# Causal attentions: queries and keys projected without padding, and spread to padded rows by a round trip through DRAM

## The chip, the cores and the metric

The kernel runs on one core of a Trainium2 chip. The metric is the device time of one execution in microseconds (us). TensorE (PE) multiplies matrices, VectorE (DVE), ScalarE (ACT) and GpSimd (POOL) do the rest of the arithmetic, and SyncE (SP) issues DMAs. Each engine runs its own instruction stream in order; semaphores order them among each other.

## The reference

The kernel computes a decoder of two layers on 16 sequences of 512 positions, with model width D = 256 and 16 heads of 16 numbers each. Every sub-layer adds its result to `x` and normalises. Layer 0: a causal self-attention with a learned position term, a cross attention to 64 context rows, and a mixture of ten experts. Layer 1: a causal self-attention with low-rank projections, a cross attention with one head, and a feed-forward part. The two causal attentions, cut to what matters:

```python
# layer 0
q, k, v = jnp.split(x @ Wqkv.T, 3, axis=-1)              # 16 heads of 16
logits = jnp.einsum('bhqd,bhkd->bhqk', q, k) * scale
logits = logits + _fourier_bias(alpha, beta, t)[None]    # sum_r alpha cos(w_r (i-j)) + beta sin(w_r (i-j))
attn = softmax(where(causal, logits, -inf)); out = (attn @ v) @ Wout.T
# layer 1
q = x @ wq_lat @ wq_heads;  k = x @ wk_lat @ wk_heads    # 256 -> 64 -> 256
att = softmax(where(causal, q k^T * SCALE, -inf));  y = (att @ v) @ w_proj + b_proj
```

The position term of layer 0 depends on i - j through cosines and sines, so it is an inner product of 16 position features of the query with 16 mixed features of the key.

## The kernel before

Everything is kept in float32 apart from masks and a split of the row maxima. The weights are loaded once; then 16 sequences pass through four stages each: `a0` (causal attention of layer 0), `d0` (first cross attention and experts), `a1` (causal attention of layer 1) and `d1` (second cross attention and feed-forward).

**Order of the work.** The code first records operations with `op(engine, cost, emit, reads, writes, wait)` (line 288): an engine, an estimated cost, and the buffers (`Slot`) they touch. `run_plan` (line 346) then lists them: at each step it takes the operation that can start earliest by its own clock, and among those that could start within 0.02 us on one engine the one with the lowest rank (line 395). The rank is the stage's place plus the fraction of its PE cost that is done, with 0.5 taken off for what touches an attention's buffers (line 325). The places (line 402) put `a1` of one sequence beside `d0` of the next, and `d1` beside `a0` of the one after, so that the dense stages fill PE while an attention waits. The plan's order is written into each engine's stream: `pe`, `dve`, `act` and `pool` are `Pinned` (line 344), which keeps the program's order on that engine. DMAs on `nc.sync` are not pinned before the change: `x`, `ctx` and `mi` are loaded by `inputs` (line 1366), and the result stored at line 1398.

**Heads and padding.** Attention scores are matmuls that contract over 32 rows of the array, one head to a strip of 32 partitions, four heads (a group) to a tile of 128 partitions. A head has 16 numbers, so 16 of 32 rows are its own; in layer 0 the other 16 hold the position features (`qfeat` for the query, a product with `kmat` for the key), in layer 1 row 16 carries the row maximum in the query and -1 in the key (`onerow`), and the rest is zero.

`queries_keys(g)` makes the two padded tiles `q` and `k` [128, 512] of group g. In `attention0` (line 825) the weight `wqk0` holds zero columns for the padding: two matmuls (two chunks of the 256 contraction rows) for the query, DVE scales it and adds `qfeat` (line 833); two matmuls and a third with `kmat` and `qfeat` (line 841) for the key, ACT copies it out. In `attention1` (line 869) one matmul each from the 64 latent rows, on the two halves of the array, with ACT scaling the query and adding the -1 row to the key. A matmul of 512 float32 columns stands in the trace as two records.

`causal_attention` (line 557) works a group in two passes: units of maxima (q against k, masked, reduced by DVE into `m`), then units of exponentials (k against q, `exp` on ACT, the triangle cut on POOL), and their products with the values. It calls `queries_keys(g)` two units of maxima ahead of the group's first (line 750); the tiles come from pools of three buffers (line 264). Its own large buffers come from `a4` with two buffers, so that one attention starts when the former is nearly done.

## Time and profile before

| | us |
|---|---|
| median of 3 runs | 4504.14 (4497.92 to 4506.57) |
| profiled execution | 4507.05 |
| its span, first to last instruction | 4505.3 |
| PE busy | 4260.3 (95%) |
| DVE busy | 2641.7 (59%) |
| ACT busy | 1571.0 (35%) |
| POOL busy | 1205.5 (27%) |
| mean granted PE clock | 0.988 of full speed |

Busy time of PE is the union of its matmuls' spans; the spans overlap in the pipeline, so what one matmul takes from the next is read from start to start. A group of instructions is named out<-in by the program's tiles: `pq` and `pk` are the PSUM tiles of the projections, `pa` the scores, `po` the products with the values, `pt` transposes, `pg`, `pu` and `pe` the experts. All recorded operations stand under line 340, the helper that pins them, so the tile names tell them apart. DMA rows give the issuing queue, how many there were, KB each, and the median time from issue to landing.

One sequence takes about 272 us in the middle of the run: its attention1 starts at 876.7, 1148.5 and 1421.9 us for three sequences in a row.

### The profile page before, as it was taken

The page shows a single profiled execution, that of the slowest core. Times are in us where ns is not written, and L with a number is a line of the kernel's source. Part 1 is how long each engine was busy: PE and PEld are TensorE (multiplying, and loading weights), DVE is VectorE, ACT ScalarE, POOL GpSimd, SP SyncE. Part 2 cuts the span into 40 slices and gives each one's busy share as a digit, 9 for nine tenths or more (in the row PEclk, how much of TensorE's full clock was granted, in tenths as well). Part 3 has the DMA queues.
Part 4 walks back from the last instruction along what each step waited for, and adds up shares of the span by engine and source line. Part 5 has one row for each costly group of instructions (what it writes and reads, how often), then busy time and mean ns, then how long its engine had stood idle before and what let it go on. Part 6 is the DMA issues. An engine that isn't in the chain of part 4 may idle for free.

```text
span 4505.3 us, 65388 instructions
## 1 busy us (share of the span) xinstructions
PE 4260.3 (95%) x26816; PEld 2372.9 (53%) x26816; DVE 2641.7 (59%) x5317; ACT 1571.0 (35%) x2273; POOL 1205.5 (27%) x2221
## 2 busy tenths in 40 slices
PE   4999999999999999999999999999999999999897
PEld 2455555555555555555555555555555555555544
DVE  2456566565666556665565665656665565655554
ACT  1323242434314243242433414343242432424333
POOL 0313231323313133131322313233131332313322
PEclk8999999999999999999999999999999999999998
DMA  4000000000000000000000000000000000000000
GB/s 129 2 1 1 2 10 2 10 1 2 10 2 10 1 2 10 2 10 1 11 1 2 10 2 10 1 2 10 2 10 1 6 6 1 10 1 6 1 1 10
DMA packets 41355, 35.05 MB, mean 8 GB/s; under 512 B 11424, under 2 KB 39904, under 8 KB 41056
## 3 DMA queue, kind: packets, MB, share of 16 engines
q1 hardware_dynamic: 30736, 23.70, 1.7%
q10 hardware_dynamic: 10320, 7.17, 0.5%
q8 instruction: 211, 3.46, 0.3%
q14 instruction: 88, 0.72, 0.1%
HBM read 22.47 MB, written 8.39 MB: 7 GB/s over the span
## 4 chain that ended last, share of the span: by engine, by line
PE 84%; ACT 6%; DVE 5%; POOL 2%; issue 1%; DMA 1%; SPq 0%; ACTq 0%; POOLq 0%; DVEq 0%
PE pa L340 22%; PE pf L340 8%; PE pq L340 7%; PE pg L340 7%; PE pe L340 6%; PE pu L340 6%; PE po L340 6%; PE pp L340 5%; PE pk L340 4%; ACT e L340 4%; PE pt L340 4%; PE ps L340 3%; PE pv L340 3%; DVE m L340 2%; PE pl L340 1%
## 5 line engine op out<-in xcount | busy, mean ns | idle before, releaser
L340 DVE TENSOR_REDUCE m<-pa 128x2 f32<-128x1024 f32 (+3 forms) x1024 | 805.6, 818 | 425.7 <-PE pa L340 423.5
L340 ACT ACTIVATE e<-pa 128x1024 f32<-128x1024 f32 (+1 forms) x768 | 662.6, 884 | 685.9 <-PE pa L340 647.7
L340 PE MATMUL pa<-q,k 32*128 32x512 f32 (+3 forms) x4096 | 665.5, 472 | 23.0 <-ACT e L340 19.7
L340 POOL TENSOR_SCALAR_AFFINE_SELECT e<-e 128x256 f32<-128x256 f32 x1024 | 437.9, 441 | 918.1 <-ACT e L340 906.8
L340 PE MATMUL pa<-k,q 32*128 32x512 f32 (+3 forms) x4096 | 616.6, 471 | 51.3 <-DVE m L340 40.2
L340 PEld LDWEIGHTS pa<-k,q 32*128 32x128 f32 x4096 | 271.4, 185 | 345.3 <-issue 155.0
L340 PEld LDWEIGHTS pa<-q,k 32*128 32x128 f32 x4096 | 297.2, 186 | 170.5 <-ACT e L340 67.3
L340 PE MATMUL po<-e,vp 128*32 128x512 f32 (+3 forms) x4096 | 360.5, 447 | 18.0 <-POOL e L340 15.9
L340 ACT ACTIVATE h<-pg 128x512 f32<-128x512 f32 x160 | 95.5, 597 | 708.2 <-PE pg L340 708.2
L340 POOL TENSOR_TENSOR rs<-rs,minus_half 128x2 f32<-128x2 f32 x192 | 133.4, 716 | 708.3 <-DVE rs L340 707.6
L340 PE MATMUL pe<-w,h 128*128 128x256 f32 x1280 | 307.6, 381 | 0.8 <-DVE h L340 0.8
L340 PE MATMUL pg<-xT,w 128*128 128x512 f32 x640 | 303.9, 597 | 0.0
L340 PE MATMUL pu<-xT,w 128*128 128x512 f32 x640 | 301.8, 594 | 0.0
L340 PEld LDWEIGHTS pe<-w,h 128*128 128x128 f32 x1280 | 240.6, 190 | 97.2 <-issue 59.0
L340 PE MATMUL pf<-xT,L_ffn_W 128*128 128x512 f32 x512 | 248.3, 610 | 0.2 <-ACT xT L340 0.2
L340 POOL CAST parts<-m 128x16 bf16<-128x16 f32 x192 | 55.2, 288 | 711.4 <-DVE m L340 703.2
L340 DVE SCALAR_TENSOR_TENSOR x<-pe,r_pick,x 128x256 f32<-128x256 f32 x512 | 215.5, 477 | 42.8 <-PE pe L340 42.8
L340 PE MATMUL pf<-ff,act 128*128 128x256 f32 x1024 | 235.7, 384 | 3.9 <-ACT act L340 3.9
L340 DVE SCALAR_TENSOR_TENSOR h<-h,pg 128x512 f32<-128x512 f32 x160 | 110.0, 687 | 197.9 <-ACT h L340 197.9
L340 PEld LDWEIGHTS <-ident 128*128 128x128 bf16 x1536 | 92.5, 97 | 245.3 <-issue 217.3
L340 PE MATMUL pa<-cmask,ident 128*128 128x128 bf16 (+1 forms) x1536 | 220.1, 242 | 0.0
L340 PEld LDWEIGHTS pf<-ff,act 128*128 128x128 f32 x1024 | 193.2, 192 | 37.4 <-ACT act L340 6.2
(180 smaller groups left out, 6359.9 us busy)
## 6 DMA issues: line engine op xcount, KB each, us to landing
x<-in_x SPq DMA_DIRECT2D x16, 512.0 KB, 3.9
out_x<-x SPq DMA_DIRECT2D x16, 512.0 KB, 2.9
wqk<-in_wqk ACTq DMA_DIRECT2D x1, 1024.0 KB, 6.0
w<-in_L_ffn_routed_w SPq DMA_DIRECT2D x8, 128.0 KB, 3.8
w<-in_L_ffn_routed_w ACTq DMA_DIRECT2D x8, 128.0 KB, 4.0
w<-in_L_ffn_routed_w ACTq DMA_DIRECT2D x1, 1024.0 KB, 9.6
L_ffn_W<-in_L_ffn_W SPq DMA_DIRECT2D x1, 1024.0 KB, 8.0
ff<-in_L_ffn_W ACTq DMA_DIRECT2D x1, 1024.0 KB, 9.0
```

The source lines that it names most:

```text
L340: return tc.keep_in_program_order(f(*args, **kw))
```

## The change

Queries and keys are projected without padding: 256 columns each in two chunks of 128 (eight heads a chunk), ordered so that row r of all eight heads lies together. In both attentions a new `spread_heads` wraps the projections. For every second group it projects a chunk of queries and keys, evicts them into tiles of two new pools, and stores each with one DMA into the first 16 of 32 rows of a DRAM tile `way[layer][query or key][chunk]` of shape [32, 8, 512]. Then each group's padded tile of 128 rows (4 heads x 32 rows) is loaded from there with one DMA. The upper 16 rows of the DRAM tiles are written once at the start: cosines and sines for the queries of layer 0, their product with the mixing matrix for its keys, zeros and a row of -1 for layer 1. Attention 0's product with `kmat` is made once at the start; `qfeat` and `onerow` go.

The projections are called four units of maxima ahead in place of two. To make room, `d4` goes from six to five buffers and `h` from three to two. SP is pinned too: the loads of `x`, `ctx` and `mi` and the store of the result take their place in the plan's order beside the new DMAs, for which the plan counts 0.6 us of SP and a wait of 2.4 us (store) or 2.8 us (load).

```diff
-    wqk0 = weight("wqk0", 2 * NG * P)
-    qfeat = const.tile([P, S], F32, tag="qfeat", name="qfeat")
-    load(qfeat, a["qfeat"])
+    wqk0 = weight("wqk0", 2 * D)
+    way = [
+        [[dram.tile([32, 8, S], F32, tag=f"way{l}{n}{c}", name="way") for c in range(NC)] for n in range(2)]
+        for l in range(2)
+    ]
+    for l, n, name in ((0, 0, "trig8"), (1, 0, "zeros8"), (1, 1, "minus8")):
+        for c in range(NC):
+            load(way[l][n][c][HD:], a[name])
...
+        for c in range(NC):
+            mixed = once_ps.tile([P, S], F32, tag="mixed", name="mixed")
+            nc.tensor.matmul(mixed, kmat[:, c * P : (c + 1) * P], trig, start=True, stop=True)
+            kfeat = once.tile([P, S], F32, tag=f"kfeat{c}", name="kfeat")
+            nc.vector.tensor_copy(kfeat, mixed)
+            load(way[0][1][c][HD:].rearrange("r h s -> (r h) s"), kfeat)
...
-    d4, h_pool, u_pool = Pool("d4", 6), Pool("h", 3), Pool("u", 1)
+    d4, h_pool, u_pool = Pool("d4", 5), Pool("h", 2), Pool("u", 1)
+    qk_pools = Pool("qh", 2), Pool("kh", 2)
...
-    pe, dve, act, pool = map(Pinned, (nc.tensor, nc.vector, nc.scalar, nc.gpsimd))
+    pe, dve, act, pool, sp = map(Pinned, (nc.tensor, nc.vector, nc.scalar, nc.gpsimd, nc.sync))
...
-            while len(groups) < NG and (n_m + 2) // 6 >= len(groups):
+            while len(groups) < NG and (n_m + 4) // 6 >= len(groups):
...
+    def spread_heads(products, layer):
+        def queries_keys(g):
+            c, tiles = g // 2, (q_pool([P, S], "q"), k_pool([P, S], "k"))
+            if g % 2 == 0:
+                for n, t in enumerate(products(c)):
+                    op(
+                        "SP", 0.6,
+                        lambda n=n, t=t: sp.dma_start(
+                            way[layer][n][c][:HD].rearrange("r h s -> (r h) s"), t.t
+                        ),
+                        [t], [("way", layer, n, c)], wait=2.4,
+                    )
+            for n, t in enumerate(tiles):
+                heads = slice(g % 2 * NG, g % 2 * NG + NG)
+                op(
+                    "SP", 0.6,
+                    lambda n=n, t=t: sp.dma_start(t.t, way[layer][n][c].rearrange("r h s -> h r s")[heads]),
+                    [("way", layer, n, c)], [t], wait=2.8,
+                )
+            return *tiles, list(tiles)
...
 # attention0, in place of queries_keys
+        def products(c):
+            both_of = []
+            for n in range(2):
+                p, t = ps_d([P, 512], "pqk"), qk_pools[n]([P, S], "qk")
+                cols = slice(n * D + c * P, n * D + (c + 1) * P)
+                PE(
+                    mm_cost(S, 2),
+                    lambda p=p, cols=cols: mm_chunks(p.t, lambda c: wqk0[:, c, cols], lambda c: xT.t[:, c]),
+                    both(xT), [p],
+                )
+                if n == 0:
+                    ACT(S, lambda p=p, t=t: act.mul(t.t, p.t, HD**-0.5), [p], [t])
+                else:
+                    ACT(S, lambda p=p, t=t: act.copy(t.t, p.t), [p], [t])
+                both_of.append(t)
+            return both_of
...
 # attention1, in place of queries_keys
+            def product():
+                pe.matmul(p.t, wqk1[0:64, cols], lat.t[0:64, 0], start=True, stop=True)
+                pe.matmul(p2.t, wqk1[64:128, cols], lat.t[64:128, 0], start=True, stop=True)
+
+            PE(mm_cost(S), product, [lat[0]], [p, p2])
             ACT(S, lambda: act.mul(q.t, p.t, HD**-0.5), [p], [q])
+            ACT(S, lambda: act.copy(k.t, p2.t), [p2], [k])
             return q, k
...
-            "SP", 0.1, lambda: nc.sync.dma_start(out[b].rearrange("(t p) d -> p t d", p=P), x.t),
+            "SP", 0.1, lambda: sp.dma_start(out[b].rearrange("(t p) d -> p t d", p=P), x.t),
```

More of the change, by code (lines that the diff above doesn't have):

```diff
@@ L93, in decoder_kernel @@
     make_identity(nc, ident)
-    wqk0 = weight("wqk0", 2 * NG * P)
-    qfeat = const.tile([P, S], F32, tag="qfeat", name="qfeat")
-    load(qfeat, a["qfeat"])
-    kmat = const.tile([P, NG * P], F32, tag="kmat", name="kmat")
-    load(kmat, a["kalpha"])
-    with tc.tile_pool(name="once", bufs=1) as once:
+    wqk0 = weight("wqk0", 2 * D)
+    dram = ctx.enter_context(tc.tile_pool(name="dram", bufs=1, space=bass.MemoryType.DRAM))
+    way = [
[5 more added lines that the diff above has]
+            load(way[l][n][c][HD:], a[name])
+    with tc.tile_pool(name="once", bufs=1) as once, tc.tile_pool(
+        name="once_ps", bufs=1, space=bass.MemoryType.PSUM
+    ) as once_ps:
+        trig = once.tile([HD, S], F32, tag="trig", name="trig")
+        load(trig, a["trig8"][:, 0])
+        kmat = once.tile([HD, D], F32, tag="kmat", name="kmat")
+        load(kmat, a["kalpha"])
         for name, op in (("kbeta", ALU.add), ("kbeta_n", ALU.subtract)):
-            part = once.tile([P, NG * P], F32, tag="part", name=name)
+            part = once.tile([HD, D], F32, tag=name, name=name)
             load(part, a[name])
             nc.vector.tensor_tensor(kmat, kmat, part, op)
+        for c in range(NC):
[4 more added lines that the diff above has]
+            load(way[0][1][c][HD:].rearrange("r h s -> (r h) s"), kfeat)
     wv0 = weight("wv0", D)
@@ L129, in decoder_kernel @@
     nc.gpsimd.memset(minus16, -1.0)
-    onerow = const.tile([P, 1], F32, tag="onerow", name="onerow")
-    load(onerow, a["onerow"])
     wq_x0 = weight("L0_xattn_wq_w", D)
@@ L169, in decoder_kernel @@
         load(wlat[:, :, n], a[f"L1_attn_{name}"].rearrange("(c p) n -> p c n", p=P))
-    wqk1 = const.tile([P, NG * P], F32, tag="wqk1", name="wqk1")
+    wqk1 = const.tile([P, D], F32, tag="wqk1", name="wqk1")
     load(wqk1, a["wqk1"])
@@ L597, in follow @@
                 )
-            return first, None, masks, follow, [q, k], [two]
+            return first, None, masks, follow, groups[g]["ready"], [two]
         def exp_unit(g, w, pair):
@@ L642, in follow @@
                 op("POOL", 0.43 * len(blocks), causal, [e], [e])
-            return first, None if exact else second, None, follow, [q, k] + ([] if exact else [groups[g]["mrow"]]), [two]
+            return first, None if exact else second, None, follow, groups[g]["ready"] + ([] if exact else [groups[g]["mrow"]]), [two]
         def spread(g):
@@ L674, in rows_of_maxima @@
             if exact:
-                DVE(S, lambda: dve.tensor_tensor(q.t, p.t, q.t, ALU.add), [p, q], [q])
+                own = [q]
+                DVE(S, lambda: dve.tensor_tensor(q.t, p.t, q.t, ALU.add), [p, *own], own)
             else:
@@ L748, in causal_attention @@
             count_m, count_e = (1, 1) if can_m and can_e else (2 * can_m, 2 * can_e)
-            while len(groups) < NG and (n_m + 2) // 6 >= len(groups):
+            while len(groups) < NG and (n_m + 4) // 6 >= len(groups):
                 g = len(groups)
-                q, k = queries_keys(g)
-                groups[g] = dict(q=q, k=k, m=small([P, NT, NG, 1], "m"))
+                q, k, ready = queries_keys(g)
+                groups[g] = dict(q=q, k=k, ready=ready, m=small([P, NT, NG, 1], "m"))
             for g in [g for g, r in rows_at.items() if r == n]:
@@ L810, in fill_values @@
         ACT(D, lambda: act.copy(vp[:, t, :, :HD], p.t[:, :D].rearrange("p (h d) -> p h d", d=HD)), [p], [("vp", t)])
+    def spread_heads(products, layer):
[18 more added lines that the diff above has]
+            return *tiles, list(tiles)
+        return queries_keys
     def attention0(x):
@@ L823, in attention0 @@
             fill_values(t, p)
-        def queries_keys(g):
-            q, k = q_pool([P, S], "q"), k_pool([P, S], "k")
-            p = ps_d([P, 512], "pq")
-            PE(
-                mm_cost(S, 2),
-                lambda: mm_chunks(p.t, lambda c: wqk0[:, c, g * P : (g + 1) * P], lambda c: xT.t[:, c]),
-                both(xT), [p],
-            )
-            DVE(S, lambda: dve.scalar_tensor_tensor(q.t, p.t, HD**-0.5, qfeat, ALU.mult, ALU.add), [p], [q])
-            p2 = ps_d([P, 512], "pk")
-            def keys():
-                for c in range(NC):
-                    pe.matmul(
-                        p2.t, wqk0[:, c, (NG + g) * P : (NG + g + 1) * P], xT.t[:, c], start=(c == 0), stop=False
-                    )
-                pe.matmul(p2.t, kmat[:, g * P : (g + 1) * P], qfeat, start=False, stop=True)
-            PE(mm_cost(S, 3), keys, both(xT), [p2])
-            ACT(S, lambda: act.copy(k.t, p2.t), [p2], [k])
-            return q, k
-        yT = causal_attention(queries_keys, False)
+        def products(c):
[14 more added lines that the diff above has]
+            return both_of
+        yT = causal_attention(spread_heads(products, 0), False)
         project_norm(x, yT, wout0)
@@ L867, in attention1, with products @@
         DVE(S, lambda: dve.tensor_copy(lat.t[:64, 1], p2.t[:64]), [p2], [lat[1]])
-        def queries_keys(g):
-            q, k = q_pool([P, S], "q"), k_pool([P, S], "k")
+        def products(c):
+            cols = slice(c * P, (c + 1) * P)
             p, p2 = ps_d([P, 512], "pq"), ps_d([P, 512], "pk")
-            cols = slice(g * P, (g + 1) * P)
-            PE(
-                mm_cost(S),
-                lambda: pe.matmul(p.t, wqk1[0:64, cols], lat.t[0:64, 0], start=True, stop=True), [lat[0]], [p],
-            )
-            ACT(S, lambda: act.mul(q.t, p.t, HD**-0.5), [p], [q])
-            PE(
-                mm_cost(S),
-                lambda: pe.matmul(p2.t, wqk1[64:128, cols], lat.t[64:128, 0], start=True, stop=True), [lat[0]], [p2],
-            )
-            ACT(S, lambda: act.activation(k.t, p2.t, AF.Identity, bias=onerow), [p2], [k])
+            q, k = (p([P, S], "qk") for p in qk_pools)
+            def product():
+                pe.matmul(p.t, wqk1[0:64, cols], lat.t[0:64, 0], start=True, stop=True)
+                pe.matmul(p2.t, wqk1[64:128, cols], lat.t[64:128, 0], start=True, stop=True)
+            PE(mm_cost(S), product, [lat[0]], [p, p2])
+            ACT(S, lambda: act.mul(q.t, p.t, HD**-0.5), [p], [q])
+            ACT(S, lambda: act.copy(k.t, p2.t), [p2], [k])
             return q, k
@@ L894, in attention1 @@
             fill_values(t, pv)
-        yT = causal_attention(queries_keys, True)
+        yT = causal_attention(spread_heads(products, 1), True)
         project_norm(x, yT, wproj)
@@ L1368, in inputs @@
         op(
-            "SP", 0.1, lambda: nc.sync.dma_start(x.t, a["x"][b].rearrange("(t p) d -> p t d", p=P)),
+            "SP", 0.1, lambda: sp.dma_start(x.t, a["x"][b].rearrange("(t p) d -> p t d", p=P)),
             (), rows_of(x), wait=6.0,
@@ L1373, in small_ones @@
         def small_ones():
-            nc.sync.dma_start(c.t, a["ctx_1024"][b])
-            nc.sync.dma_start(mi.t, a["mask_BxS2_ik0"][b].partition_broadcast(P))
+            sp.dma_start(c.t, a["ctx_1024"][b])
+            sp.dma_start(mi.t, a["mask_BxS2_ik0"][b].partition_broadcast(P))
         op("SP", 0.1, small_ones, (), [c, mi], wait=4.0)
@@ L1425, in _laid_out, with by_rows @@
     wqkv = np.asarray(i["L0_attn_Wqkv"]).T
-    qk = z((D, 2, H, 32), np.float32)
-    qk[:, :, :, :HD] = wqkv[:, : 2 * D].reshape(D, 2, H, HD)
-    a["wqk0"] = qk.reshape(D, -1)
+    def by_rows(w):
+        return w.reshape(len(w), NC, 8, HD).transpose(0, 1, 3, 2).reshape(len(w), D)
+    a["wqk0"] = np.concatenate([by_rows(wqkv[:, :D]), by_rows(wqkv[:, D : 2 * D])], 1)
     a["wv0"] = wqkv[:, 2 * D :]
     a["wout0"] = np.asarray(i["L0_attn_Wout"]).T
-    heads = z((2, 64, H, 32), np.float32)
-    heads[0, :, :, :HD] = np.asarray(i["L1_attn_wq_heads"]).reshape(64, H, HD)
-    heads[1, :, :, :HD] = np.asarray(i["L1_attn_wk_heads"]).reshape(64, H, HD)
-    a["wqk1"] = heads.reshape(P, -1)
+    a["wqk1"] = np.concatenate([by_rows(np.asarray(i[f"L1_attn_w{n}_heads"])) for n in "qk"])
     R = HD // 2
@@ L1438, in _laid_out @@
     angle = omega[:, None] * np.arange(S)[None, :]
-    trig = z((4, 32, S), np.float32)
-    trig[:, 16:24], trig[:, 24:32] = np.cos(angle), np.sin(angle)
-    a["qfeat"] = trig.reshape(P, S)
+    trig = np.concatenate([np.cos(angle), np.sin(angle)]).astype(np.float32)
+    a["trig8"] = np.repeat(trig[:, None], 8, 1)
     alpha, beta = np.asarray(i["L0_attn_alpha"]), np.asarray(i["L0_attn_beta"])
-    ka, kb, kn = (z((P, H, 32), np.float32) for _ in range(3))
+    ka, kb, kn = (z((HD, H, HD), np.float32) for _ in range(3))
     for r in range(R):
-        cos, sin = 16 + r, 24 + r
+        cos, sin = r, R + r
         ka[cos, :, cos] = ka[sin, :, sin] = alpha[:, r]
         kb[cos, :, sin] = kn[sin, :, cos] = beta[:, r]
-    a["kalpha"], a["kbeta"], a["kbeta_n"] = (k.reshape(P, -1) for k in (ka, kb, kn))
+    a["kalpha"], a["kbeta"], a["kbeta_n"] = (by_rows(k.reshape(HD, -1)) for k in (ka, kb, kn))
+    a["zeros8"], a["minus8"] = z((2, HD, 8, S), np.float32)
+    a["minus8"][0] = -1.0
     p = np.arange(P)
@@ L1451, in _laid_out @@
     a["vmask"] = (p[:, None] // SK == np.arange(2 * HD)[None, :] // HD).astype(np.float32)
-    a["onerow"] = -(p % 32 == HD).astype(np.float32)[:, None]
     a["prio"] = np.tile(np.arange(NE, 0, -1, dtype=np.float32), (P, 1))
```

## The prediction

> **What bounds the kernel now.** I read the page's busy times first, then the matmul groups by shape with what they waited for, then PE in order of time across the places where one attention gives way to the next, and last the DMA issues.

> The page's first part and the stages of one sequence (columns: stretch, its length, busy time of PE, its weight loads, DVE, ACT, POOL; then granted clock, DMA share, GB/s):

> ```profile
> PE 4260.3 (95%) x26816; PEld 2372.9 (53%) x26816; DVE 2641.7 (59%) x5317; ACT 1571.0 (35%) x2273; POOL 1205.5 (27%) x2221
> ```

> ```profile
> 967.00:1045.00 78.00, 78.00 (x312) 44.92 (x311) 51.68 (x118) 10.59 (x20) 4.92 (x11) 1.00 0.00 1
> 1045.00:1143.00 98.00, 94.46 (x671) 53.80 (x670) 51.81 (x110) 45.88 (x62) 33.79 (x69) 1.00 0.01 2
> 1143.00:1160.00 17.00, 16.20 (x83) 7.48 (x81) 11.95 (x30) 6.60 (x13) 6.32 (x10) 1.00 0.19 63
> 1160.00:1236.00 76.00, 71.37 (x592) 37.07 (x593) 46.76 (x70) 34.42 (x46) 30.25 (x50) 0.98 0.00 1
> ```

> PE is the bound, and steadily: no idle time in the stage where the experts run beside the start of attention0, 4.6 us of 76 where attention1 runs beside the first cross attention. DVE has room, DMA is nearly idle. So a matmul taken away is worth its time, as long as no new wait takes its place.

> What a projection costs is read from start to start, since the 592 ns of one record include the pipeline. PE in order of time at the head of an attention0, then of an attention1:

> ```profile
> 970.64 1.88 PE L340 MATMUL pq<-xT,wqk 128*128 128x512 f32 x4
> 972.36 1.88 PE L340 MATMUL pk<-xT,wqk 128*128 128x512 f32 x4
> 974.08 1.02 PE L340 MATMUL pk<-qfeat,kmat 128*128 128x512 f32 x2
> 974.93 1.88 PE L340 MATMUL pq<-xT,wqk 128*128 128x512 f32 x4
> 976.74 1.14 PE L340 MATMUL pa<-k,q 32*128 32x512 f32 x8
> ```

> ```profile
> 1148.47 0.69 PE L340 MATMUL pq<-lat,wqk 64*128 64x512 f32 x1
> 1148.48 0.69 PE L340 MATMUL pk<-lat,wqk 64*128 64x512 f32 x1
> ...
> 1149.57 2.42 PE L340 MATMUL pv<-wv,lat 64*128 64x256 f32 x8
> 1151.92 1.14 PE L340 MATMUL pa<-k,q 32*128 32x512 f32 x8
> ```

> One attention0 group takes 1.72 + 1.72 + 0.85 = 4.29 us. In attention1 the two halves of the array work at once: about 1.0 us for a pair, though one pair in four runs one after the other (1.90 us from 1154.28 to 1156.18). In both, scores follow the first projection within 4 us. The DMA rows (KB each, median us from issue to landing):

> ```profile
> out_x<-x SPq DMA_DIRECT2D x16, 512.0 KB, 2.9
> ctx<-in_ctx SPq DMA_DIRECT2D x16, 64.0 KB, 2.2
> qfeat<-in_qfeat SPq DMA_DIRECT2D x1, 256.0 KB, 3.3
> kbeta<-in_kbeta SPq DMA_DIRECT2D x1, 256.0 KB, 6.6
> wqk<-in_wqk SPq DMA_DIRECT2D x1, 256.0 KB, 2.9
> L_xattn_Wq<-in_L_xattn_Wq SPq DMA_DIRECT2D x1, 256.0 KB, 6.3
> L_xattn_Wv<-in_L_xattn_Wv SPq DMA_DIRECT2D x1, 256.0 KB, 7.6
> ```

> **The change part by part**, against the profiled run's 4507.05 us (span 4505.3; 2.9 above the median of 4504.14).

> *Attention0's projections.* Before, 4 groups x 4.29 = 17.2 us of PE a sequence. After, two chunks of queries and keys without the feature matmul, 2 x 2 x 1.72 = 6.9. Saved: 10.3 x 16 = **165 us**. Most of it lies where PE is never idle, so it counts whole.

> *Attention1's projections.* Before, 1.10 + 0.96 + 1.90 + 1.06 = 5.0 us a sequence (first, second, third, fourth group); after, two pairs at 1.0 (far end 1.9 each): saved 3.0 (1.2), so 48 us (19). This stage has small waits of PE for DVE and ACT that less filler lets grow, so I count three quarters: **36 us**.

> *Evictions.* DVE loses 64 x 692 ns, ACT 64 of about 640 ns, both beside PE and in no chain that ends last: 0. The value of the -1 row and of the position rows now comes by DMA, which costs no engine.

> *The way through DRAM.* New on SP, a sequence and layer: 4 stores and 8 loads of 256 KB, each some 0.4 us of issue (the 0.37 to 0.47 of SP's rows): 16 x 2 x 12 x 0.4 = 154 us of a queue that now only waits. The loads for groups 1 to 3 are issued one to several score steps early and PE passes some 11 us of other work meanwhile (first scores of the first group at 1151.9, of the second at 1163.1): 0; without that cover each would cost what the first does. The first group's cannot be early. From the end of k's eviction: store between 2.2 and 2.9 (64 KB and 512 KB rows), taken 2.6; an issue 0.4; load between 2.9 and 7.6 (the 256 KB rows). I take 6.5, the middle of the ten 256 KB rows of the SP queue (6.3 and 6.6), because q, k and the next group's pair go out back to back, as those did. Together 9.5 us. The planner allows 0.6 + 2.4 + 0.6 + 2.8 and two hops of 0.06: 6.5. PE's order is fixed by the plan, so PE stands before the scores for what its filler doesn't cover.
> At attention1's head (1148.5): k is evicted at 1150.8, tiles at 1160.3. PE has the values until 1152, the other chunk until 1153, then cross0's transposes (x normalised at 1152.1 on DVE), a 0.6 us gap for their eviction, and its query projections until 1158.2: 2.1 + 0.6 = 2.7 us lost. At attention0's head (1240.6): keys projected by 1247.5, evicted 1248.1, tiles at 1257.6; PE has the second chunk until 1250.9, then the experts' transposes, router and first gate (x ready 1249.7) until about 1255.5: 2.4 us with the eviction gap. Sum (2.7 + 2.4) x 16 = **+82 us**; with loads of 2.9 us about 10, with 7.6 about 117.

> On how many DMA engines share a load, no row shows such a shape. [...]

> *Waits on SP.* Before, SP sat for hundreds of us in front of the loads of mi and the stores of out_x; now these stand in the plan's order with the new DMAs behind them. The plan issues each when its buffer or rows are due, so I cost it at 0; a store that is 5 us late would hold the next group's loads as long, 16 times, 80 us at most.

> *Buffers.* h 3 to 2, d4 6 to 5: 0. In the expert stage pe of one expert already precedes pg of the second after it; in cross0 the fourth score tile already starts after the second one's transposes (1199.5 against 1197.2). Were that order lost, one 0.6 us eviction for each of ten experts: 96 us.

> *Start.* 2 MB of position rows, zeros and -1 to DRAM, some 1.6 MB of weights less, at 256 to 280 GB/s: 1.5 us; two stores that wait for a matmul in the load queues, 3; attention0's first head with little to fill it, 5: **+10 us** (0 to 20).
> PE's granted clock was 0.72 between 80 and 100 us, with PE busy 16.5 of 20, and 1.00 in nearly all later stages. [...]

> Sum: 4507 - 165 - 36 + 82 + 10 = 4398, or 4395 on the median's scale.

> **Rivals.** *Hidden altogether*: loads land near 2.9 us, as wqk did, and attention1 gives all of its 48: 4504 - 165 - 48 + 10 + 10 = 4311. For it: DMA share is 0.00 to 0.01 outside the start, so nothing competes. Against it: q, k and the next pair compete with one another.
> *The pair's loads queue behind each other* (the other side): at each of 32 heads the second lands 13 us after issue instead of 6.5, 32 x 6.5 = 208 us more, 4600. It decides from 3.4 us more a head (109 / 32), where all is lost. For it: 256 KB rows of 7.4 to 7.6 with several in flight. Against: those shared the engines with far more traffic.
> *The freed time turns into waits*: an attention's chain of maxima, exponentials and values sets the pace, PE's waits for DVE m and ACT e (43.3 + 29.3 us in the view of waits) more than double, 4395 + 85 = 4480. Against it: 78 of 78 busy in the expert stage, DVE at 59%.

> **How the numbers follow.** Forecast 0.47 (own range 4340 to 4460), hidden 0.20, queued loads 0.22, waits 0.11. Changes under 0.2%, 9 us, can't be told from none. Faster: 0.47 + 0.20 + half of the waits, 0.72; same 0.06 (some of the queued and waiting cases); slower 0.22. The range runs from the hidden case to just short of the queued one, 4305 to 4570.

> **What would show it.** 256 matmul records from xT and attention0's wqk in place of 512, no kmat matmul per group; PE busy about 200 us less; a new wait of PE's pa for a DMA of q or k, some 32 times, 2 to 3 us each. If those waits are 6 us or more, or come with groups 1 to 3 too, the forecast is wrong on the slow side; if they are missing, on the fast side; if PE's waits for DVE m and ACT e grow instead, the third rival holds.

## The result and the profile after

The changed kernel takes 4707.83 us (median of 4 runs, 4702.23 to 4712.75) against 4501.74 for the kernel before (median of 4): ratio 1.0457, 95% interval 1.0439 to 1.0475. The profiled execution spans 4703.2 us, 198 more than before. The forecast was 4395, and 4570 the upper end of its range. In the three later sessions, of the runs e1 to e11, the kernel before took 4497 to 4501 us; each ratio is to the kernel before of its own session. One of e6's four runs took 6873 us at a granted clock of 0.551, the others 4534 to 4538; the median given there counts all four.

The page's first part and its chain of work, by engine and by tile (shares of the span):

```profile
PE 4243.3 (90%) x26308; PEld 2386.2 (51%) x26308; DVE 2611.5 (56%) x5255; ACT 1535.5 (33%) x2209; POOL 1198.8 (25%) x2221
...
PE 73%; DMA 9%; DVE 7%; ACT 6%; POOL 2%; issue 2%; SPq 0%; ACTq 0%; POOLq 0%; DVEq 0%
PE pa L358 22%; PE pf L358 8%; DMA k<-way 7%; PE pu L358 6%; PE pe L358 6%; PE po L358 6%; PE pg L358 6%; PE pp L358 4%; DVE m L358 3%; PE pt L358 3%; PE ps L358 3%; ACT e L358 3%; PE pv L358 2%; PE pq L358 2%; PE pqk L358 2%
```

508 matmul records are gone, yet PE's busy time fell by only 17 us: what is left runs slower, since the clock is lower. The chain now has a DMA in it, the load of the padded keys. The middle of the run, before and then after (columns: stretch, length, busy time of PE, its weight loads, DVE, ACT, POOL; then granted clock, DMA share, GB/s):

```profile
300.00:2000.00 1700.00, 1637.63 (x10330) 910.27 (x10328) 1033.37 (x2075) 604.26 (x876) 466.04 (x849) 1.00 0.02 5
```

```profile
300.00:2000.00 1700.00, 1566.72 (x9717) 881.17 (x9715) 982.11 (x1981) 551.20 (x800) 434.70 (x802) 0.95 0.08 27
```

Idle time of PE went from 62 to 133 us here, and the granted clock from 1.00 to 0.95. The views of waits (us in total, times, longest), PE's before, PE's after and SP's after:

```profile
PE pa L340 <- DVE m L340: 43.3, 92, 1.5
```

```profile
PE pa L358 <- DMA k<-way: 159.3, 38, 7.3
PE pa L358 <- DVE m L358: 97.4, 112, 2.6
```

```profile
SPq L358 <- DMA way<-qk: 290.6, 90, 9.0
```

The wait for the keys is new, and the one for DVE's maxima has more than doubled. PE in order of time at the head of an attention1, and SP beside it:

```profile
1202.02 2.32 PE L358 MATMUL pv<-wv,lat 64*128 64x256 f32 x8
...
1206.76 3.70 PE L358 MATMUL pq<-xT,L_xattn_wq_w 128*128 128x512 f32 x8 [0.21 <-ACT xT L358]
1216.46 2.09 PE L358 MATMUL pa<-k,q 32*128 32x512 f32 x8 [6.00 <-DMA k<-way]
```

```profile
1202.71 0.32 SPq L358 DMA_DIRECT2D way<-qk  x1
1203.08 0.43 SPq L358 DMA_DIRECT2D out_x<-x  x1
1203.61 0.51 SPq L358 DMA_DIRECT2D way<-qk  x1
1204.84 1.14 SPq L358 DMA_DIRECT2D q<-way  x2
1207.31 1.08 SPq L358 DMA_DIRECT2D k<-way  x2
1208.48 1.00 SPq L358 DMA_DIRECT2D way<-qk  x1
1209.54 0.54 SPq L358 DMA_DIRECT2D x<-in_x  x1
```

PE stands for 6.0 us, and then its first scores take 2.09 us where they took 1.14 before. At the next attention0's head the wait is 3.86 us, and the scores again take 2.09. (In the middle of the run these waits are 5.6 to 6.4 us at attention1's heads and 3.4 to 3.9 at attention0's.)

```profile
1309.74 7.03 PE L358 MATMUL pqk<-xT,wqk 128*128 128x512 f32 x16
1316.61 1.99 PE L358 MATMUL pt<-ident,x 128*128 128x128 f32 x16
...
1326.06 2.09 PE L358 MATMUL pa<-k,q 32*128 32x512 f32 x8 [3.86 <-DMA k<-way]
```

SP issued both groups' queries (1204.84, two DMAs) ahead of the first keys, since the query's store lands first; x and the second chunk's stores follow at once. The same microseconds as windows, same columns as above:

```profile
1205.00:1206.00 1.00, 1.00 (x8) 0.53 (x6) 0.00 (x0) 0.60 (x1) 0.00 (x0) 1.00 1.07 361
...
1208.00:1209.00 1.00, 1.00 (x3) 0.38 (x2) 0.00 (x0) 0.22 (x1) 1.00 (x2) 1.00 0.26 98
...
1214.00:1215.00 1.00, 0.00 (x0) 0.00 (x0) 0.00 (x0) 0.00 (x0) 0.00 (x0) 1.00 0.56 208
1215.00:1216.00 1.00, 0.00 (x0) 0.00 (x0) 0.00 (x0) 0.00 (x0) 0.00 (x0) 0.59 0.27 102
...
1224.00:1225.00 1.00, 1.00 (x3) 0.49 (x2) 1.00 (x2) 0.00 (x0) 0.00 (x0) 0.50 0.26 92
```

Two things are to be seen. With stores in flight the DMA share is about 1; with only loads of the padded tiles in flight it is 0.26, as much as 4 of the 16 engines, at 98 GB/s, so 256 KB take 2.6 us and several loads stand in line. And after nearly 5 us without a matmul the granted clock falls to 0.50 at 1215 and stays there for 10 us.

### An account by idle time and clock

For several kernels I cut the run from 200 us to about 100 us before the end into stretches of 2 us and added up two things: PE's idle time, and length x (1 - granted clock) over the stretches whose clock was under 0.97, with adjoining ones taken as one drop. The two overlap where PE idles at half clock, so their sum is an upper bound. "e" names are those of the experiments below.

| kernel | clock drops | time lost to the clock, us | PE idle, us |
|---|---|---|---|
| before | 8 | 27 | 155 |
| after | 53 | 228 | 352 |
| e1, loads on 16 engines | 29 | 114 | 232 |
| e2, other order on SP | 45 | 179 | 291 |
| e3, loads wait for no store | 9 | 26 | 124 |
| e4, matmuls in the gap | 36 | 118 | 238 |
| e6, e1 with an early head | 49 | 229 | 223 |
| e9, middle groups only | 20 | 67 | 176 |
| e10, those of attention0 only | 28 | 106 | 171 |
| e11, e9 on 4 engines | 41 | 143 | 247 |

Before to after, the table has 197 us more idle and 200 us more lost to the clock. Without the overlap, and over the whole profiled span, PE idles 215 us more, loses 176 us more (half of its busy time at half clock), and its busy time, as it would be at full clock, falls by 194: together the 198 us between the two profiled executions. Counted from start to start, each moment for the matmul that started last, attention0's projections fell by 169 us and attention1's by 43, and 19 us came on top in other groups.

### The profile page after: what moved, and what is told of

Its sections match the earlier page's. It is cut to its first block, busy times and chain, and to the rows that moved or that the text cites. A ratio compares the mean times of both kernels' runs of the same rounds, so it can differ in the third digit from the quotient of the medians.

```text
span 4703.2 us, 65393 instructions
## 1 busy us (share of the span) xinstructions
PE 4243.3 (90%) x26308; PEld 2386.2 (51%) x26308; DVE 2611.5 (56%) x5255; ACT 1535.5 (33%) x2209; POOL 1198.8 (25%) x2221
## 4 chain that ended last, share of the span: by engine, by line
PE 73%; DMA 9%; DVE 7%; ACT 6%; POOL 2%; issue 2%; SPq 0%; ACTq 0%; POOLq 0%; DVEq 0%
PE pa L358 22%; PE pf L358 8%; DMA k<-way 7%; PE pu L358 6%; PE pe L358 6%; PE po L358 6%; PE pg L358 6%; PE pp L358 4%; DVE m L358 3%; PE pt L358 3%; PE ps L358 3%; ACT e L358 3%; PE pv L358 2%; PE pq L358 2%; PE pqk L358 2%
## 5 line engine op out<-in xcount | busy, mean ns | idle before, releaser
L358 PE MATMUL pa<-k,q 32*128 32x512 f32 (+3 forms) x4096 | 695.5, 528 | 252.0 <-DMA k<-way 159.3
L358 PE MATMUL pa<-q,k 32*128 32x512 f32 (+3 forms) x4096 | 690.7, 483 | 33.3 <-ACT e L358 23.9
L358 PEld LDWEIGHTS pa<-k,q 32*128 32x128 f32 x4096 | 308.6, 205 | 544.7 <-issue 316.6
L358 PE MATMUL po<-e,vp 128*32 128x512 f32 (+3 forms) x4096 | 358.8, 445 | 19.1 <-POOL e L358 17.2
L358 PE MATMUL pu<-xT,w 128*128 128x512 f32 x640 | 324.7, 632 | 0.3 <-ACT yT L358 0.3
L358 PE MATMUL pa<-cmask,ident 128*128 128x128 bf16 (+1 forms) x1536 | 238.8, 259 | 0.0
## 6 DMA issues: line engine op xcount, KB each, us to landing
way<-qk SPq DMA_DIRECT2D x128, 256.0 KB
q<-way SPq DMA_DIRECT2D x128, 256.0 KB
k<-way SPq DMA_DIRECT2D x128, 256.0 KB
x<-in_x SPq DMA_DIRECT2D x16, 512.0 KB
out_x<-x SPq DMA_DIRECT2D x16, 512.0 KB
```

The costliest lines, as they stand in the source:

```text
L358: return tc.keep_in_program_order(f(*args, **kw))
```

## The experiments

The theory after the result: the change loses its saving at the heads of the attentions, where the first scores wait for tiles that 4 DMA engines carry and that stand behind other transfers. The rivals: the order on SP; the buffers and the pinned SP queue; and that the removed projections were needed as filler, wherever the tiles come from.

### e1: the same loads on sixteen engines

```diff
-        [[dram.tile([32, 8, S], F32, tag=f"way{l}{n}{c}", name="way") for c in range(NC)] for n in range(2)]
+        [[dram.tile([8, 32, S], F32, tag=f"way{l}{n}{c}", name="way") for c in range(NC)] for n in range(2)]
-                            way[layer][n][c][:HD].rearrange("r h s -> (r h) s"), t.t
+                            way[layer][n][c].rearrange("h r s -> r h s")[:HD], t.t
-                    lambda n=n, t=t: sp.dma_start(t.t, way[layer][n][c].rearrange("r h s -> h r s")[heads]),
+                    lambda n=n, t=t: sp.dma_start(t.t, way[layer][n][c][heads].rearrange("h r s -> (h r) s")),
```

> The DRAM tiles are laid out with the head outermost, [8, 32, 512], so that a group's 128 rows are contiguous for the load; stores and loads move the same bytes at the same places of the plan, and PE's order is that of the changed kernel. Theory (loads that occupy a quarter of the DMA engines, as the DMA share of 0.25 to 0.27 during them shows, land late; PE waits, and its clock is then halved): DMA share near 1 and some 0.7 us of transfer a load in place of 2.6, PE's waits for k<-way fall from 159 us to under 40, clock back above 0.975, total 4330 to 4430. Rival (the two DMA latencies in series are too long whatever the engines): waits of 2 us or more remain at each of 32 heads, clock stays near 0.95, total 4550 to 4680.

Measured: 4499.16 us, ratio to before 1.0003 (0.9989 to 1.0018); clock 0.967. So some 209 us, as much as the whole loss, hang on the layout of a DRAM tile alone; PE, DVE and POOL run the same instructions in the order of the changed kernel. From 1163 to 1164 us in e1, with the next loads in flight, the DMA share is 1.08 at 393 GB/s, where the same loads of the changed kernel have 0.26 at 98. The total lies between the theory's range and the rival's. PE's waits, then one head of attention1 in e1, and the same head in the kernel before:

```profile
PE pa L358 <- DVE m L358: 101.9, 127, 2.5
PE pc L358 <- DMA ctx<-in_ctx: 34.6, 1, 34.6
PE pa L358 <- DMA k<-way: 29.7, 17, 3.4
```

```profile
1159.44 0.59 PE L358 MATMUL pq<-lat,wqk 64*128 64x512 f32 x1
...
1162.02 3.70 PE L358 MATMUL pq<-xT,L_xattn_wq_w 128*128 128x512 f32 x8 [0.21 <-ACT xT L358]
1167.38 1.14 PE L358 MATMUL pa<-k,q 32*128 32x512 f32 x8 [1.66 <-DMA k<-way]
...
1181.14 2.27 PE L358 MATMUL pa<-k,q 32*128 32x384 f32 x16 [1.11 <-DVE m L358]
1183.34 0.61 PE L358 MATMUL pa<-cmask,ident 128*128 128x256 bf16 x4
1186.41 1.22 PE L358 MATMUL pa<-k,q 32*128 32x256 f32 x4 [2.46 <-DVE m L358]
```

```profile
1153.32 0.69 PE L340 MATMUL pq<-lat,wqk 64*128 64x512 f32 x1
...
1161.20 1.94 PE L340 MATMUL pq<-xT,L_xattn_wq_w 128*128 128x512 f32 x4
```

```profile
1180.00:1183.00 3.00, 1.89 (x13) 1.17 (x14) 3.00 (x4) 0.97 (x1) 1.90 (x1) 1.00 0.00 0
1183.00:1186.00 3.00, 0.95 (x10) 0.50 (x6) 3.00 (x4) 0.09 (x1) 1.90 (x1) 0.82 0.00 0
1186.00:1189.00 3.00, 2.59 (x8) 1.07 (x8) 2.69 (x5) 1.06 (x1) 1.24 (x2) 0.50 0.00 0
```

The keys' wait is down from 159.3 to 29.7 us. But e1 only comes back to the time before, although PE's work at full clock is 178 us less: over the whole span PE idles 88 us more and loses 79 more to the clock, and the wait for DVE's maxima is 59 us above that of the kernel before. The windows of e1 show one place: DVE is busy all of 1180 to 1186, on maxima and on the cross attention's softmax, and PE waits for it in gaps of 1.11 and 2.46 us. The clock falls within the second, at 1184.9.

What PE lacks there can be read from the order. In the kernel before, the next groups' projections (1153.32) and the cross attention's query projections (1161.20) come after the first scores of 1151.92, between maxima. In e1 they lie ahead of the first scores (1159.44 to 1165.72), where they cover the round trip, and are missing afterwards. This is argued from the order; no run changes it by itself.

### e2: a group's own keys ahead of the next group's queries

```diff
-                    [("way", layer, n, c)], [t], wait=2.8,
+                    every if g % 2 else [every[n]], [t], wait=2.8,
 # every = [("way", layer, n, c) for n in range(2)]: the second group's loads come after both stores
```

> The loads of a second group (q and k of the next four heads) are put behind both stores of the chunk, so that SP issues k of the first group before q of the second; same DRAM layout, same order on PE. [...] Rival (the series of store and load latency, not the queue): waits and total unchanged, 4690 to 4720.

Measured: 4607.81 us, 1.0245 (1.0219 to 1.027), still with loads on 4 engines; PE waits 95.3 us for the keys where it was 159.3, not the unchanged total and waits of the rival. The order on SP alone is worth some 100 us of the 206. How far these 100 and e1's 209 overlap isn't settled: the two edits together ran only with an early head (e8, below), where 4533 against 4537 us shows no difference clear of the noise.

### e3: loads that wait for no store

```diff
+    still = dram.tile([32, 8, S], F32, tag="still", name="still")
-                    lambda n=n, t=t: sp.dma_start(t.t, way[layer][n][c].rearrange("r h s -> h r s")[heads]),
-                    [("way", layer, n, c)], [t], wait=2.8,
+                    lambda n=n, t=t: sp.dma_start(t.t, still.rearrange("r h s -> h r s")[heads]),
+                    (), [t], wait=2.8,
```

> The padded tiles are loaded from a DRAM tile that is written once at the start with zeros, so the loads no longer depend on the stores (which go on) and the plan puts them as early as buffers allow; the queries and keys that reach the scores are zeros, so the projections' results are left out of the attention. All work of PE, evictions and DMA bytes stay. Both theories of a late arrival: waits for k<-way under 20 us, clock 0.98 or more, the saving of PE shows whole: total 4290 to 4390. Rival (the freed time turns into waits for DVE and ACT, or the clock falls for another reason): 4480 or more with few waits for DMA.

Measured: 4255.69 us, 0.9452 (0.9428 to 0.9476); clock 0.989, PE busy 4022.6. With the same projections, stores and 4-engine loads, but no dependence between them, the kernel is 241 us faster than before. That is better than the 4290 to 4390 expected. So the work that the prediction took off PE is really gone (PE's work at full clock is 232 us less), and the loads' traffic and their four engines cost little at most as long as nobody waits for them. The missing work does not by itself bring waits for DVE's maxima either, which are below the 43.3 us of the kernel before:

```profile
PE pa L361 <- DVE m L361: 29.6, 65, 2.5
```

Two things besides the wait differ here. The plan's order is another one, since loads can go early and no score needs a projection any more, so that the projections may stand wherever PE is free. And the scores are computed on zeros; whether that matters to the clock no run shows.

### e4: matmuls in the gap

```diff
+            if n == 0:
+                spare = ps_d([P, 512], "spare")
+                def busy(spare=spare):
+                    for _ in range(5):
+                        pe.matmul(spare.t, ident, wqk0[:, 0, :S], start=True, stop=True)
+                PE(0.01, busy, groups[0]["ready"], [spare])
```

> The changed kernel, with five matmuls of constants (0.86 us each, 4.3 us, results unused) in front of the first scores of each of the 32 attentions, where PE waits for the loads anyway. Theory (the wait lets the clock drop to half for some 10 us, which costs about 5 us a head beside the wait): clock back to 0.975 or more, waits for k<-way fall by most of 4.3 us a head, total 4530 to 4600 though more work is done. Rival (the clock drop costs little, the wait alone is the loss): the matmuls fill part of the wait or lengthen it, total 4700 to 4760.

Measured: 4645.91 us, 1.0323 (1.0301 to 1.0344); clock 0.967 against 0.943 in the changed kernel. Five more matmuls an attention, which nobody reads, make the changed kernel 62 us faster. The total lies between the 4530 to 4600 expected and the rival's 4700 to 4760. The tiles land no sooner for them: from the issue of the keys' load to the first scores it is 9.1 us (1193.38 to 1202.49) at a head of attention1, against 9.2 in the changed kernel.

```profile
1193.38 1.10 SPq L358 DMA_DIRECT2D k<-way  x2
```

So at least these 62 us were lost to the clock and not to the wait itself. By the account the clock costs 110 us less than in the changed kernel, of which the added matmuls take a part back.

### e5: the rest of the change alone

The kernel before, with the smaller pools, the lead of four units and SP in the plan's order:

```diff
-    d4, h_pool, u_pool = Pool("d4", 6), Pool("h", 3), Pool("u", 1)
+    d4, h_pool, u_pool = Pool("d4", 5), Pool("h", 2), Pool("u", 1)
-    pe, dve, act, pool = map(Pinned, (nc.tensor, nc.vector, nc.scalar, nc.gpsimd))
+    pe, dve, act, pool, sp = map(Pinned, (nc.tensor, nc.vector, nc.scalar, nc.gpsimd, nc.sync))
-            while len(groups) < NG and (n_m + 2) // 6 >= len(groups):
+            while len(groups) < NG and (n_m + 4) // 6 >= len(groups):
```

> The kernel before with only the side edits of the change: d4 with five buffers, h with two, queries_keys called four units of maxima ahead, SP pinned to the plan's order; projections padded and on chip as before. The prediction's step (these cost nothing): within 0.4% of the kernel before, 4480 to 4515. Rival (they make part of the 206 us): 4530 or more.

Measured: 4499.82 us, 1.0005 (0.9995 to 1.0015). Within that interval this part of the change costs nothing, beside padded projections; with the new ones it wasn't tried alone.

### e6, e7, e8: the head projected earlier

Could the round trip be covered by an earlier start? The latent and projected tiles get pools of their own and a rank 0.1 of a stage earlier, so that the projections and stores lie well ahead of the first scores (e6 on e1's layout, e7 on the change's, e8 with e2's order on e1's layout):

```diff
-    a4 = Pool("a4", 2)
+    a4, xa = Pool("a4", 2), Pool("xa", 2)   # xT and lat of the attentions come from xa
-    qk_pools = Pool("qh", 2), Pool("kh", 2)
+    qk_pools = Pool("qh", 1), Pool("kh", 1)
+            if any(s.pool.name in ("xa", "qh", "kh") for s in o.slots):
+                ahead = 0.5 + 0.1
             o.rank = place + done / total - ahead
```

> The sixteen-engine layout, and the head of an attention is let start earlier: the transposed input and the latent rows come from a pool of their own (two buffers) instead of the attention's pool of two, the pools of evicted chunks go from two buffers to one to make room, and what touches these ranks 0.1 of a place earlier. The same work on every engine, in another order. Theory (what is left of the loss with sixteen engines is the round trip at the 32 heads, which the plan can't cover because a head may only start when the former attention has let go of its buffers): waits for k<-way under 15 us, clock 0.98 or more, total 4260 to 4360. Rival (what is left is queueing of DMAs or the order of the dense stages): total 4430 to 4500.

> The same early head as in the run with sixteen engines, but on the changed kernel's DRAM layout, whose loads run on four engines. Theory (the slow loads cost only where PE stands before them; with the head covered they are hidden): within 60 us of the run with sixteen engines and the early head, 4270 to 4420. Rival (four engines are too slow for the whole stream of loads, covered or not): 4500 or more, with waits for k<-way over 80 us.

> Sixteen engines, the early head, and a second group's loads put behind both stores of its chunk, so that SP issues k of the first group before q of the second. If loads still queue at the heads: up to 30 us faster than the early head with sixteen engines. If the heads are covered already: within 15 us of it.

Measured: e6 4536.6 us, 1.0086 (1.0069 to 1.0103); e7 4546.52, 1.011 (1.0095 to 1.0125); e8 4533.05, 1.008 (1.0065 to 1.0095). In e6 PE waits for the keys once, 0.5 us, and it is 37 us slower than e1, above both ranges of its expectation: my theory that an uncovered round trip is what e1 still lacks has fallen. e6's longest waits of PE, and PE in order of time:

```profile
PE pa L360 <- DVE m L360: 98.0, 88, 3.3
PE pa L360 <- ACT e L360: 40.9, 48, 1.1
PE pt L360 <- DVE x L360: 36.4, 23, 7.1
PE pa L360 <- DMA k<-way: 0.5, 1, 0.5
```

```profile
1253.39 0.61 PE L360 MATMUL pa<-cmask,ident 128*128 128x256 bf16 x4
1257.25 2.42 PE L360 MATMUL pa<-k,q 32*128 32x256 f32 x8 [3.25 <-DVE m L360]
```

Here scores with no projection between them run into DVE's maxima: the clock falls within the gap of 3.25 us and is at half from 1257 to 1271. What is worse than in e1 is the clock: 49 drops for 29 and 229 us lost for 114, with 9 us less idle time. PE's wait for the maxima itself is no longer (98.0 for 101.9); those for ACT's exponentials (40.9 for 26.5) and for DVE's normalised x (36.4 for 22.8) are. And e7 against e6 is 10 us, with 10.2 us of waits for the keys: four engines cost next to nothing where the loads are covered. e7's total, as e6's, lies above the range expected.

### e9, e10, e11: only the middle groups through DRAM

If the head needs its projections, they may as well be padded there. In e9 groups 0 and 3 of each attention are projected padded, as before; groups 1 and 2, one chunk of eight heads, go through DRAM with contiguous loads, asked for six units ahead, with `d4` and `h` back at six and three buffers. e10 does so in attention0 only, attention1 being all padded. e11 is e9 with the DRAM tiles laid out as in the change.

```diff
+            if g in [0, 3]:
+                q, k = q_pool([P, S], "q"), k_pool([P, S], "k")
+                padded([0, 3].index(g), q, k)       # the projections of the kernel before
+                return q, k, [q, k]
-            while len(groups) < NG and (n_m + 4) // 6 >= len(groups):
+            while len(groups) < NG and (n_m + 6) // 6 >= len(groups):
 # e11 alone, against e9: way is [32, 8, S], as in the change
```

> The first and the last group of each attention are projected padded as before the change (4.29 us of PE a group in attention0, 1.0 in attention1); only the two groups in the middle go through DRAM as one chunk of eight heads, with contiguous loads, projected at the head, 6 units of maxima ahead. Nothing waits for a DMA at an attention's head. PE work a sequence: attention0 17.2 to 2 x 4.29 + 3.44 = 12.0, attention1 5.0 to 3.0, 16 x 7.2 = 115 us less than before. Theory (what the change lost is the round trip in front of the first scores, and the half clock that these gaps bring): the saving lands almost whole, 4385 to 4420, ratio 0.975 to 0.982, granted clock 0.98 or more, no PE wait for way's loads over 10 us in all. Rival (the removed projections were filler where DVE's maxima pace the head, wherever the tiles come from): waits for DVE m near 100 us, clock under 0.97, 4470 to 4510.

> The same for attention0 alone; attention1 is projected padded for all four groups as before the change. Work a sequence 5.2 us less, 16 x 5.2 = 83 us. Theory: 4417, and about 30 us above the kernel that has both. Rival (in attention1 the projections are filler that is missed): not slower than the kernel that has both, 4385 to 4400.

> The kernel with both middle groups through DRAM, on PE, DVE and POOL instruction for instruction the same, but with the DRAM tiles laid out as in the change, so that a load runs on 4 of 16 engines (2.6 us for each of four loads behind one another, 10.4 us, and 2.6 for the store). Group 1's scores come six units of maxima, some 12 us, after the first; theory: a slow load that is covered costs little, within 25 us of the contiguous one, with PE waits for the loads under 30 us. Rival (the four engines cost by themselves, by what they hold up): over 60 us more, as from 4499 to 4708 in the change.

Measured: e9 **4418.87 us, 0.9818 (0.9802 to 0.9835)**; e10 4468.4, 0.9927 (0.9911 to 0.9944); e11 4536.09, 1.0072 (1.0054 to 1.009). The same head in e9, and then in e11 its wait, SP and two windows of half a microsecond (columns as above):

```profile
1132.55 1.14 PE L369 MATMUL pa<-k,q 32*128 32x512 f32 x8
...
1137.89 3.60 PE L369 MATMUL pq<-xT,L_xattn_wq_w 128*128 128x512 f32 x8
...
1143.95 1.14 PE L369 MATMUL pa<-k,q 32*128 32x512 f32 x8 [0.60 <-DVE m L369]
```

```profile
1174.51 2.09 PE L369 MATMUL pa<-k,q 32*128 32x512 f32 x8 [4.59 <-issue]
```

```profile
1162.30 1.40 SPq L369 DMA_DIRECT2D way<-qk  x2
1164.38 1.15 SPq L369 DMA_DIRECT2D q<-way  x2
1165.62 1.28 SPq L369 DMA_DIRECT2D k<-way  x2
```

```profile
1166.00:1166.50 0.50, 0.50 (x2) 0.19 (x1) 0.50 (x1) 0.12 (x1) 0.00 (x0) 1.00 0.26 102
1173.00:1173.50 0.50, 0.00 (x0) 0.00 (x0) 0.00 (x0) 0.00 (x0) 0.00 (x0) 0.50 0.27 106
```

e9 is 82 us faster than before, where its work is 115 less: by the account 21 us more idle and 40 more lost to the clock ate part. (115 less these 61 is 54. Over the whole span PE's work at full clock fell by 157 us: the projections by 116, as counted, the scores by 27, the rest in smaller groups.) No wait for a tile from DRAM is left, as expected, and PE waits 16.8 us for DVE's maxima. e10 gains 32 of its 83 us, where 4417 was expected, and is 50 above e9, so attention1's part helps and isn't filler that is missed. It is more than the 32 us of work between the two; the account has 39 us more lost to the clock in e10, and why is open. e11 went against my expectation: 117 us slower than e9, with PE's, DVE's and POOL's instructions the same. I had counted 12 us of cover from the first scores to group 1's. But the store could only start at 1162.3, after the chunk's eviction, the four loads then ran one after the other from 1165.5 to 1176 (10.5 us, 4 x 2.6), and PE was out of other work at 1169.9. It stood 4.59 us, and the clock dropped. ("issue" means that the profile shows no releaser; by 3 x 2.6 us the third load of the line, group 1's keys, is through at about 1173.4, so it is taken for the wait.) Such waits come to 81 us in 17 places (47.2 under "issue", 34.1 under the keys). By the account e11 idles 71 us more than e9 and loses 76 more to the clock. So four engines cost by the wait and the clock after it, as e3 and e7 show from the other side, and the cover has to be counted from the store's issue and against the whole line of loads.

## Why the prediction was wrong

**The step that failed: the way through DRAM, +82 us, and with it the clock, for which the sum has no term.** The waits for the keys came to 159.3 us where the sum had 82, and the clock after them and after other gaps to 176 us where it had nothing. PE's other idle time grew by 56 us. With 212 us of projections gone and 19 us of other work on top, that is the 198 us by which the profiled execution is longer.

*The wait.* The prediction priced a load at 6.5 us from issue, by 256 KB rows of the trace before. None of these was a load in four slices, and the text said so. In the runs the share with such loads alone in flight was 0.26, as much as 4 engines of 16, and each took 2.6 us of transfer. What was too small in the sum was the line: in front of the first group's keys stood the next group's queries, and behind them x and the second chunk's stores were in flight too (DMA share 0.56 to 1.09 in the windows from 1210 to 1215). From the issue of the keys' load to the first scores it was 9.2 us (1207.3 to 1216.5), not 6.5, and the gaps were 6.00 and 3.86 us where the sum had 2.7 and 2.4.

*The clock.* This was the larger error. The sum has gaps of 2.7 and 2.4 us at the heads and counts nothing for the clock after them. No run shows that gaps of this length leave the clock alone: at the attention0 head above it fell at 1324.4, 2.2 us into the gap (0.71 in the window from 1324 to 1325, 0.50 in the next), and in e1 after a gap of 1.11 us and the first 0.9 us of the next. At attention1's heads the gaps grew to 5.6 to 6.4 us. Each drop lost some 4.3 us (228 / 53). The trace before shows one already: PE waited 0.78 us up to 1177.46, and then

```profile
1176.00:1178.00 2.00, 1.22 (x10) 0.62 (x10) 1.28 (x2) 1.35 (x2) 2.00 (x3) 0.94 0.00 0
1178.00:1180.00 2.00, 2.00 (x18) 1.02 (x14) 1.23 (x3) 1.15 (x2) 1.55 (x3) 0.50 0.03 8
```

**Rival 2, loads in line (0.22), had the place and the cause of the wait right**, but not its size: it had 82 + 208 = 290 us of waits for 159. The waits came 77 us above the sum, 2.4 us a head, and by its own account it decides only from 3.4. With 56 us of other idle time and 19 of other work, the waits bring the change back to even, 22 us above the kernel before; the 176 us beyond that are the clock, which no rival counted. **Rival 3 (freed time turns into waits)** holds in part beside it: PE's waits for DVE's maxima and ACT's exponentials grew from 72.6 to 124.0 us, short of the doubling that it named, and in e6, with next to no wait for the keys, waits for engines and the clock take the whole saving. **Rival 1 (hidden)** shows in e3: 4256 without the dependence, where it had 4311. In e6 it is hidden and the loss is elsewhere.

**The projections, -165 and -36: the work went.** The four projections of attention0 take 6.87 us (1309.74 to 1316.61) for the 6.9 of the sum, all of attention0's fell by 169 us and all of attention1's by 43, and e3 gives back all of it. "So it counts whole" was too quick: in e1 PE does 178 us less and gains nothing, because other waits and the clock take it. **Buffers, lead and the pinned SP: 0**, shown by e5. **SP's waits at 0** was wrong where its queue is shared, for the order of its loads was worth some 100 us (e2). Not how long SP waits matters (290.6 us for stores to land here, 284.1 in e2), but what stands ahead of the first keys. **Start, +10:** the first scores come at 83.2 us in place of 69.4, 7.35 us of them a wait for the keys: 14 us, inside its bounds of 0 to 20.

## What to carry to other kernels

A round trip through DRAM costs the work that must stand still until it is back, so count its cover from the store's issue, over all transfers in line, and read in the DMA share how many engines a load really uses; the DRAM tile's layout alone was worth 209 us here. Other work that is moved ahead to cover a wait is missing where it stood; look there for new waits (so I read the order of e1; no run shows it alone). e9, which leaves the heads as they were, kept 82 of its 115 us. On PE a gap has a second price, the half clock after it, here 4.3 us a drop; price a new wait with it.

## What the runs showed of the hardware

What stays open is why e6's early head brings 49 drops of the clock where e1 has 29, since its edit moves the whole plan, and what an order with more room for DVE between the maxima would give.
